# Cross-attention keys of a Perceiver layer: transposes on TensorE replaced by transposing DMA transfers

## Chip, core and metric

The kernel runs on one core of a Trainium2 chip. A core has five engines, each with its own instruction queue: TensorE (PE; its weight loads are listed as PEld), VectorE (DVE), ScalarE (ACT), GpSimd (POOL) and SyncE (SP), which here issues nearly all DMA transfers. Sixteen DMA engines move data between HBM, where the inputs lie, and SBUF, the on-chip memory of 128 partitions. TensorE writes to PSUM, eight banks of 128 x 512 float32. The metric is the device time of one execution in microseconds (us).

## The reference, cut to what matters

Everything is float32. `x` is (16, 64, 256), the context `cond` is (16, 1601, 256). A layer runs three residual parts: a block with self attention and cross attention, a second small block-local attention with its feed-forward, and a gated feed-forward. The change touches the cross attention of the first part:

```python
qx = _fp8_linear_pertensor(ln_out, wqx, wqx_scale, qx_in_scale).reshape(b, s, g, hpg, d)
qx = _ln(qx, qxln_w, qxln_b)
kvx = jnp.einsum('bsi,oi->bso', cond, w_kv_x)
kx, vx = jnp.split(kvx, 2, axis=-1)
kx = _ln(kx.reshape(b, sc, g, d), kxln_w, kxln_b)
vx = vx.reshape(b, sc, g, d)
xout = _gqa(qx, kx, vx).reshape(b, s, nh * d)
```

There are 16 query heads and g = 8 key groups of d = 128. `_ln` is a layer norm over d with weight and bias; `_gqa` is softmax(q k / sqrt(d)) v, two heads to a key group.

## The kernel before

**Tiles and units.** The 1,024 rows of `x` make 8 tiles of 128 rows, two batches each (`NT = 8`). The cross attention of one tile (i), one half of the key groups (hh, four of them) and one batch (bb) is a *unit*: 32 units in all. A unit walks through the 1,601 context rows in 13 chunks of 128 (`NC = 13`); the last one is a tail of 65, and the tails of both batches of a tile are projected together. `unit` (line 541) writes every step of a chunk as a small function and puts it into a heap with `at(step, rank, fn)`; the heap is then emptied in the order of (step, rank). Units start 13 steps apart, so that one step holds about one chunk of scores of one unit and one chunk of sums of the unit before it. Self attention, queries, output projections and the last two parts of the layer are generators, which are spawned at steps of their own, with waits in `PACE` and `SCHEDULE`. That gives the order of the program; the framework's planner then fills each engine's queue from it, by priority and by its own estimates of times. `behind` (line 493) adds an order between two VectorE instructions by hand.

**One chunk.** `load_T` loads context columns, two chunks at a time. `project` (line 564) makes keys of four groups, 128 x 512, in PSUM (`ps_k`; L568, two passes of two matmuls), and ScalarE squares them (L502). The weights have been centred, so the mean of a key is zero. `squares` sums the squares on VectorE (L507), then GpSimd adds epsilon (L190) and takes the power -0.5 (L191). `normalise` multiplies the keys by these roots on VectorE into SBUF (`kn`, L514). `transpose_k` turns the four 128 x 128 blocks on TensorE (L589, into `tr_kx`), and ScalarE copies them to SBUF as `kT`, with the layer norm's weight and bias, which are per partition there (L598). `score` multiplies with the queries `qx` (L606), ScalarE scales the scores into `P` (L611), and VectorE keeps a running maximum `M` (L616). At the unit's end `maximum` turns and reduces `M` (L623 to L633), and a DMA through a DRAM row brings it back to all partitions (`rowd`, L635, L652). About 18 steps after the first, the second half of a chunk's work starts: subtract the maximum (L656), exponential (L660), and `accumulate`, which multiplies the probabilities with the raw context (`ctxN`, L561; L675). The value projection follows later in `pair_out`.

**Queries.** `queries` (line 382) makes four heads of one tile at a time through `heads` (line 364): projection, layer norm, four transposes (L376), and one ScalarE pass with weight and bias into `qx` (L377).

**Other lines named below.** L897 is a GpSimd product in the last parts; L922 loads `near` keys there, 16 transfers in a row; L272 rounds weights at the start; L1062 is an activation of 128 columns with a scale per row; L368 copies a projection from PSUM.

Buffers: two PSUM tiles for projections (`mm`), three for scores, transposes and everything else (`s`), three for sums; three `kT`, 18 `P`, ten weight pieces (`w`).

Of the kernel before, what the change touches and what calls it, by code (L numbers as in the profile page):

```python
# [42 lines left out]
    0: (-9, [4, 11, 16, 25], [-3, -3, 11, 21]),  # L43
    1: (27, [36, 45, 61, 69], [37, 50, 62, 74]),
}
# [5 lines left out]
    "ln": [-1, 0.5, 0.5, -1, 1.5, -1.5, -4.5, 1.5],  # L51
    "last": [0, 0, 0, 0, 0, 0, 0, 2, -1, 0, 2, -1.5, -0.5, -0.5, -0.5, -0.5, 0, 0, 0, 0, 0.5, -0.5, -1, 1, 0, 0.5, -0.5, 0.5, -1, 0, 0, -1],
    "quarter": [-2, 3.5, 2, 1.5],
    "pair": [0, 0, 1, 1, 0, 1],
    "ln_first": [0, 0, 0, 1, 0, -0.5, -2.5, 1.5],
    "last_tile": [-1.5, 0.5, 0, 1, 0, 1.5, -2, -0.5, 0.5, 0.5, 0, 0.5, -1.5, 0.5, -0.5, 1, -1, 1, -0.5, 0, 0, 0, -1, 3, 0, 1.5],
}


# [12 lines left out]
def body(tc, ctx, a):  # L72
# [30 lines left out]
    def fact(*k):  # L103
        facts[k] = facts.get(k, 0) + 1
# [58 lines left out]
    pscale = const.tile([P, 1], F32, tag="pscale", name="pscale")  # L163
    V.tensor_tensor(pscale, col("p_in"), col("p_w"), ALU.mult)
    rows = const.tile([P, 3, H], F32, tag="rows", name="rows")
    shp = const.tile([P, 32 + 8], F32, tag="shp", name="shp")
# [149 lines left out]

    xqs, qxs = {}, {}

# [44 lines left out]

    def heads(xq, ws, scale, scale_sq, lw, lb, out_t):
        ps = s_tile("ps_q")
        project(ps, xq, ws, 0, 512)
        qn = qp.tile([P, 512], F32, tag="qn", name="qn")
        A.copy(qn, ps)  # L368
        yield 1
        st = norm_stats(qn, 4, D, scale=scale, scale_sq=scale_sq)  # L370
        yield 1
        norm_apply(qn, qn, st, 4, D)
        yield 1
        tr = tr_tile("tr_q")
        for h in range(4):
            PE.transpose(tr[:, h * P : (h + 1) * P], qn[:, h * P : (h + 1) * P], ident)  # L376
        A.activation(  # L377
            out_t().rearrange("p b h s -> p h b s"), tr.rearrange("p (h b s) -> p h b s", h=4, b=2),
            AF.Identity, bias=lb, scale=lw,
        )  # L380

    def queries(i, p):

        ws = weights("wqx", p) if i else [raw_piece("wqx", p)]
        yield 2
        if p % 2 == 0:
            qxs[i, p // 2] = qp.tile([P, 2, 8, S], F32, tag="qx", name="qx")
        out = qxs[i, p // 2]
        yield from heads(
            xqs[i][3], ws, col("wqx_s"), wsq[:, 3:4], col("qxln_w"), col("qxln_b"),  # L390
            lambda: out[:, :, 4 * (p % 2) : 4 * (p % 2) + 4, :],
        )
        fact("qx", i, p // 2)


# [97 lines left out]
    def behind(ins, other):  # L493
# [4 lines left out]
        )  # L498

    def square(ps, n):  # L500
        sq = one.tile([P, 512], F32, tag="sq", name="sq")
        A.activation(sq[:n], ps[:n], AF.Square)  # L502
        return sq

    def roots(sq, n):
        ss = small.tile([P, 4], F32, tag="ss", name="ss")
        mark["ss"] = V.reduce_sum(ss[:n], sq[:n].rearrange("p (g d) -> p g d", g=4), axis=AX.X)  # L507
        rs = small.tile([P, 4], F32, tag="rsx", name="rsx")
        rsqrt(rs[:n], ss[:n], 1.0 / D, 4)
        return rs  # L510

    def normalised(ps, rs, n):
        kn = one.tile([P, 512], F32, tag="kn", name="kn", bufs=2)
        mark["kn"] = V.tensor_tensor(  # L514
            kn[:n].rearrange("p (g d) -> p g d", g=4), ps[:n].rearrange("p (g d) -> p g d", g=4),
# [4 lines left out]
    def last_keys(hh):  # L520
# [12 lines left out]
        for g in range(4):  # L533
            PE.transpose(tr[:, g * P : g * P + B], kn[:B, g * D : (g + 1) * D], ident[:B, :B])
        A.activation(
            k_last[:, hh], tr.rearrange("p (g t) -> p g t", g=4)[:, :, 0:B],
            AF.Identity, bias=col("kxln_b"), scale=col("kxln_w"),
        )
        fact("k_last", hh)

    def unit(i, hh, bb, base):
        b = 2 * i + bb
        last = b == B - 1 and hh == 1
        st = {"cxT": {}, "cxN": {}, "ps": {}, "ss": {}, "rs": {}, "kn": {}, "kT": {}, "P": {}, "pT": {}}
        pair = pairs.setdefault((i, hh), {})
# [18 lines left out]
        def project(c):  # L564
            n, o = P, (c % 2) * P
            ps = ps_mm.tile([P, 512], F32, tag="mm", name="ps_k")
            for k in range(2):
# [3 lines left out]
                )  # L571
            st["ps"][c], st["ss"][c] = ps, square(ps, n)

        def squares(c):
            st["rs"][c] = roots(st["ss"].pop(c), P)

        def normalise(c):
            kn = normalised(st["ps"].pop(c), st["rs"].pop(c), P)

            for name in ("M", "mx"):  # L580
                if name in mark:
                    behind(mark["kn"], mark[name])
            st["kn"][c] = kn

        def transpose_k(c):
# [4 lines left out]
            if c < NC - 1:  # L590
                kT = st["kT"][c] = kp.tile([P, 4, P], F32, tag="kT", name="kT")
                out, src = kT, tr.rearrange("p (g t) -> p g t", g=4)
            else:
                need(1, "k_last", hh)
                kT = pair["kT"] = one.tile([P, 4, 2, TAIL], F32, tag="kT_tail", name="kT_tail")
                GP.tensor_copy(kT[:, :, :, REST], k_last[:, hh, :, b : b + 2])
                out, src = kT[:, :, :, 0:REST], tr.rearrange("p (g e t) -> p g e t", g=4, e=2)
            A.activation(out, src, AF.Identity, bias=col("kxln_b"), scale=col("kxln_w"))  # L598

        def score(c):  # L600
# [4 lines left out]
            for g in range(4):  # L605
# [3 lines left out]
                )  # L609
            pc = pp.tile([P, 512], F32, tag="P", name="P")  # L610
            A.activation(pc[:n], ps[:n], AF.Copy, scale=C_ATT)  # L611
            if c == 0:
                st["M"] = one.tile([P, 512], F32, tag="M", name="M")
                mark["M"] = V.tensor_copy(st["M"], pc)
            else:
                mark["M"] = V.tensor_tensor(st["M"][:n], pc[:n], st["M"][:n], ALU.max)  # L616
            st["P"][c] = pc

# [8 lines left out]

        def out_rows(r):

            tr = tr_tile("tr_r")  # L630
            PE.transpose(tr[0:4, 0:P], r, ident)
            rT = small.tile([4, P], F32, tag="rT", name="rT", bufs=2)
            A.copy(rT, tr[0:4, 0:P])  # L633
            d = dram.tile([4, P], F32, tag="rowd", name="rowd", bufs=4)
            nc.sync.dma_start(out=d, in_=rT)  # L635
            return d

        def maximum():
            r = turned("M", ALU.max)
            if not last:  # L640
                st["mxd"] = out_rows(r)
                return
# [11 lines left out]
        def exponent(c):  # L654
            n, pc = rows_of(c), st["P"][c]
            ins = V.tensor_tensor(pc[:n], pc[:n], st["mx"][:n].rearrange("p g q -> p (g q)"), ALU.subtract)  # L656
            for name in ("kn", "ss"):
                behind(ins, mark[name])
            mark["mx"] = ins
            A.activation(pc[:n], pc[:n], AF.Exp)  # L660
# [31 lines left out]
        def turn_contexts(k):  # L692
# [7 lines left out]
            fact("pc", i, hh)  # L700

        for c in range(NC):
            if c < NC - 1 or bb == 0:
                if c % 2 == 0:
                    at(base + c - 5, 0, lambda c=c: load_T(c))
                at(base + c, 1.1, lambda c=c: project(c))
                at(base + c, 6.2, lambda c=c: squares(c))
                at(base + c + 1, 2.5, lambda c=c: normalise(c))
                at(base + c + 1, 8.9, lambda c=c: transpose_k(c))
            at(base + c + 2, 8.9, lambda c=c: score(c))  # L710
            at(base + c + 17, 0, lambda c=c: load_N(c))
            at(base + c + 18, 8.4, lambda c=c: exponent(c))
            at(base + c + 20, 0.1, lambda c=c: accumulate(c))
        at(base + 15, 8.9, maximum)
        if not last:
            at(base + 17, 0.1, maximum_in)
        for k in range(2):
            at(base + 33, (1.6, 6.2)[k], lambda k=k: turn_contexts(k))

# [8 lines left out]

    FILL = {"pair": 5, "norm": 1, "sc0": 2, "sc1": 4, "av0": 1, "hn": 1, "quant2": 1, "xn": 1}

# [138 lines left out]
    def last_parts(i, start):  # L869
# [55 lines left out]
        def product(out, x, y, order):  # L925

            t = one.tile([P, 1024], F32, tag="b2b", name="prod")
            V.tensor_tensor(t.rearrange("p (h j d) -> p h j d", h=8, j=8), x, y, ALU.mult)
# [213 lines left out]
    for i in range(NT):  # L1142
        base = 52 * i
        for hh in range(2):
            for bb in range(2):
                unit(i, hh, bb, base + 26 * hh + 13 * bb)
            spawn(base + 26 * hh + 13 + 34 - 2 + (2, 2)[hh], 6.0, paced("pair", pair_out(i, hh, 3 if i < NT - 1 or hh == 0 else None)))
        ln0, sa0, qx0 = SCHEDULE[i] if i in SCHEDULE else (
            base - 22, [base + o for o in (-15, -2, 7, 21)], [base + o for o in (-17, -6, 11, 17)]
        )  # L1150
        spawn(ln0, 3.6, paced("ln" if i else "ln_first", ln_tile(i)))
        for p in range(4):
            spawn(sa0[p] - 2, 2.0, paced("sa", self_attention(i, p)))
            spawn(qx0[p] - 2, 4.0, paced("qx", queries(i, p)))
        l0 = base + {NT - 3: 96, NT - 2: 85, NT - 1: 79}.get(i, 91)
        spawn(l0, 0.6, paced("last" if i < NT - 1 else "last_tile", last_parts(i, l0)))
    spawn(60, 5.7, ternary())
# [76 lines left out]
```

## Time and profile before

| what | value |
|---|---|
| time, median of 2 runs | 2552.14 us (2551.69 to 2552.58) |
| profiled execution, time | 2552.61 us |
| its span on the core | 2550.8 us |
| granted TensorE clock, mean | 0.993 of full speed |
| transposes of keys on TensorE (L589) | 1,600, busy 241.0 us |
| scores (L606), full chunks | 3,072, busy 407.3 us |
| sums (L675) | 4,160, busy 807.6 us |
| projections (L568) | 1,600, busy 759.4 us |
| HBM read and written | 337.94 and 25.23 MB, 142 GB/s over the span |

How to read it: the busy time of an engine is the time in which at least one of its instructions was under way. A group's row gives its line, engine, operation, the names of what it writes and reads, shapes, count, busy time, mean ns of one instruction, and then the idle time of the engine just before them with what ended it. "Issue" is time in which an engine waited for nothing that the profile shows. The chain is the work that ended last, followed back from the last instruction. The sequencer's queue of an engine has a q behind its name (SPq). In the slices each digit is a tenth of busy share in one fortieth of the span.

### The profile page before, as it was taken

Reading aid. Unit: us, or ns where it says so; the run is one execution under the profiler, and the core shown is the slowest. Engines: PE = TensorE matmul, PEld = TensorE weight load, DVE = VectorE, ACT = ScalarE, POOL = GpSimd, SP = SyncE. Lnnn points to the kernel's source line nnn. Section 1 sums busy time; section 2 is a strip of 40 time slices with the busy share of each in tenths; the row PEclk is TensorE's granted clock in tenths of the full one; section 3 lists DMA queues with packets and bytes.
Section 4 is the critical chain, followed back from the end, with each engine's and each line's share of the span. In section 5 each row is a group of like instructions: output and inputs, shape, how many; then the busy total and the mean of one; then the engine's idle time right before and its main releaser. Section 6 shows DMA issues by size and latency. Waiting matters only on the chain.

```text
span 2550.8 us, 40365 instructions
## 1 busy us (share of the span) xinstructions
PE 2489.9 (98%) x14009; PEld 1927.3 (76%) x14009; DVE 1857.2 (73%) x4491; ACT 1327.9 (52%) x2444; POOL 944.0 (37%) x1225
## 2 busy tenths in 40 slices
PE   6999999999999999999999999999999999999995
PEld 3677777777777777877778777777777777777784
DVE  6777767678767786577866777677876777766755
ACT  3655545454574555645556554545454455555431
POOL 3434333343333433334333443334433343333300
PEclk8999999999999999999999999999999999999998
DMA  7655725434544354433543435343363334532333
GB/s 248 201 187 182 273 70 183 144 112 141 170 146 130 103 175 143 156 123 115 179 146 127 134 110 185 126 136 105 104 219 123 121 114 128 168 107 61 124 115 104
DMA packets 223587, 365.85 MB, mean 143 GB/s; under 512 B 31676, under 2 KB 159896, under 8 KB 223384
## 3 DMA queue, kind: packets, MB, share of 16 engines
q1 hardware_dynamic: 222840, 362.57, 43.3%
q8 instruction: 112, 1.84, 0.3%
q10 hardware_dynamic: 544, 0.69, 0.1%
q14 instruction: 91, 0.75, 0.1%
HBM read 337.94 MB, written 25.23 MB: 142 GB/s over the span
## 4 chain that ended last, share of the span: by engine, by line
PE 83%; DVE 9%; POOL 4%; DMA 1%; issue 1%; ACT 1%; SPq 1%; DVEq 0%; POOLq 0%; ACTq 0%
PE acc L675 25%; PE ps_k L568 23%; PE s L606 12%; PE tr_kx L589 6%; PE po_p L309 2%; PE ps_q L358 2%; PE po_x L746 2%; POOL rsx L191 2%; POOL ve L190 1%; DVE ss L507 1%; PE tr_pc L698 1%; PE sc L440 1%; DVE kn L514 1%; PE ps_kv L358 1%; PE pgu L1058 1%
## 5 line engine op out<-in xcount | busy, mean ns | idle before, releaser
L675 PE MATMUL acc<-ctxN,P 128*128 128x257 f32 (+5 forms) x4160 | 807.6, 340 | 0.1
L568 PE MATMUL ps_k<-wkx,ctxT 128*128 128x512 f32 x1600 | 759.4, 596 | 9.8 <-DVE wkx L1129 6.8
L675 PEld LDWEIGHTS acc<-ctxN,P 128*128 128x128 f32 (+1 forms) x4160 | 689.6, 190 | 84.5 <-issue 14.3
L190 POOL TENSOR_SCALAR ve<-ss 128x4 f32<-128x4 f32 (+1 forms) x418 | 253.3, 606 | 1281.0 <-DVE ss L507 1079.6
L502 ACT ACTIVATE sq<-ps_k 128x512 f32<-128x512 f32 x402 | 240.1, 597 | 692.7 <-PE ps_k L568 688.1
L191 POOL TENSOR_TENSOR rsx<-ve,nhalf 128x4 f32<-128x4 f32 x402 | 484.3, 1205 | 31.6
L606 PEld LDWEIGHTS s<-qx,kT 128*128 128x128 f32 x3072 | 387.5, 192 | 61.9 <-issue 51.7
L568 PEld LDWEIGHTS ps_k<-wkx,ctxT 128*128 128x128 f32 x1600 | 274.3, 192 | 201.5 <-issue 188.7
L514 DVE TENSOR_TENSOR kn<-ps_k,rsx 128x512 f32<-128x512 f32 x402 | 275.8, 686 | 193.6 <-POOL rsx L191 191.9
L606 PE MATMUL s<-qx,kT 128*128 128x128 f32 x3072 | 407.3, 275 | 0.0
L507 DVE TENSOR_REDUCE ss<-sq 128x4 f32<-128x512 f32 x402 | 273.7, 681 | 156.0 <-ACT sq L502 153.4
L660 ACT ACTIVATE P<-P 128x512 f32<-128x512 f32 (+1 forms) x416 | 261.4, 630 | 137.0 <-DVE P L656 135.8
L611 ACT ACTIVATE P<-s 128x512 f32<-128x512 f32 (+1 forms) x416 | 248.1, 596 | 146.2 <-PE s L606 138.6
L598 ACT ACTIVATE kT<-tr_kx,vec 128x512 f32<-128x512 f32 x384 | 296.7, 773 | 7.7 <-PE tr_kx L589 7.7
L656 DVE TENSOR_TENSOR P<-P,mx 128x512 f32<-128x512 f32 (+1 forms) x416 | 282.3, 680 | 0.0
L616 DVE TENSOR_TENSOR M<-P,M 128x512 f32<-128x512 f32 (+1 forms) x384 | 261.8, 682 | 15.7 <-ACT P L611 15.0
L589 PE MATMUL tr_kx<-ident,kn 128*128 128x128 f32 x1600 | 241.0, 273 | 8.3 <-DVE kn L514 4.1
L589 PEld LDWEIGHTS tr_kx<-ident,kn 128*128 128x128 f32 x1600 | 187.7, 142 | 11.5 <-issue 5.1
L209 DVE TENSOR_SCALAR qn<-qn,mv,rs 128x128 f32<-128x128 f32 x256 | 73.9, 342 | 84.0 <-POOL rs L203 83.9
L191 POOL TENSOR_TENSOR rs<-ve,nhalf 128x4 f32<-128x4 f32 (+2 forms) x144 | 116.0, 806 | 8.9
L190 POOL TENSOR_SCALAR ve<-mv,wsq 128x4 f32<-128x4 f32 (+1 forms) x96 | 38.1, 397 | 127.8 <-DVE mv L200 127.6
L309 PE MATMUL po_p<-wproj,cat 128*128 128x256 f32 x512 | 83.5, 306 | 0.6 <-ACT qn L368 0.5
(203 smaller groups left out, 2439.9 us busy)
## 6 DMA issues: line engine op xcount, KB each, us to landing
wproj<-wproj SPq DMA_DIRECT2D x120, 512.0 KB
ctxT<-in_ctx SPq DMA_DIRECT2D x192, 256.0 KB
ctxN<-in_ctx_n SPq DMA_DIRECT2D x384, 128.0 KB
wq<-wq SPq DMA_DIRECT2D x56, 512.0 KB
wkv<-wkv SPq DMA_DIRECT2D x56, 512.0 KB
wqx<-wqx SPq DMA_DIRECT2D x56, 512.0 KB
near<-kv SPq DMA_DIRECT2D x248, 64.0 KB
wvx<-in_w_kv_x SPq DMA_DIRECT2D x16, 512.0 KB
```

What stands on the lines that cost most here:

```text
L190: GP.tensor_scalar(ve[:n, :g], in_, scale, EPS, ALU.mult, ALU.add)
L191: GP.tensor_tensor(out, ve[:n, :g], nhalf[:n, :g], ALU.pow)
L507: mark["ss"] = V.reduce_sum(ss[:n], sq[:n].rearrange("p (g d) -> p g d", g=4), axis=AX.X)
L514: mark["kn"] = V.tensor_tensor(kn[:n].rearrange("p (g d) -> p g d", g=4), ps[:n].rearrange("p (g d) -> p g d", g=4), rs[:n].unsqueeze(2).t ...
L568: PE.matmul(ps[:n, :], lhsT=st["cxT"][c // 2][:, k, o : o + n], rhs=wkx[:, k, 512 * hh : 512 * (hh + 1)], start=k == 0, stop=k == 1,)
L589: PE.transpose(tr[:, g * P : (g + 1) * P], kn[:, g * D : (g + 1) * D], ident)
L598: A.activation(out, src, AF.Identity, bias=col("kxln_b"), scale=col("kxln_w"))
L606: PE.matmul(ps[:n, g * P : (g + 1) * P], lhsT=kT[:, g, 0:n], rhs=qxs[i, hh][:, bb, 2 * g : 2 * g + 2, :].rearrange("p h s -> p (h s)"), st ...
L616: mark["M"] = V.tensor_tensor(st["M"][:n], pc[:n], st["M"][:n], ALU.max)
L656: ins = V.tensor_tensor(pc[:n], pc[:n], st["mx"][:n].rearrange("p g q -> p (g q)"), ALU.subtract)
L660: A.activation(pc[:n], pc[:n], AF.Exp)
L675: PE.matmul(ps, lhsT=pc[:n, g * P : (g + 1) * P], rhs=cx[:n, o : o + w], start=g == 2 and c == 0, stop=c == NC - 1 and (g, o) in ((2, 0), ...
```

## The change

Keys are no longer normalised and turned on the way to the scores. For all units but the first and the last (`DIRECT = (1, 1)`), the raw projected keys are copied from PSUM as two planes of 16-bit halves (`split_keys`, ScalarE), stored to DRAM (`store`, 256 KB a chunk), and loaded back by a transposing DMA (`turn`, 256 KB), which writes both halves beside each other, so that the result read as float32 is the turned key. Projections of these units run one step earlier (`LEAD = 1`), tails three. The first and last unit copy the raw keys and turn them on TensorE as before. Since keys are raw, the roots multiply the scores: ScalarE's copy of 512 columns becomes four of 128 columns with a scale per row. The tail is still normalised, then split and turned by DMA (15 of 16).

The key weight goes into the queries' layer norm (`qk`), and the key bias becomes a term per query: `biases` computes it from the normalised queries (a GpSimd product, a VectorE sum), `out_rows` turns it to rows and stores it to DRAM (32 times), and `bias_in` spreads it over partitions once per unit. `biased` adds it to every chunk of scores on GpSimd, before the running maximum, which gets a function and a later step of its own. The roots' epsilon is scaled so that 1/sqrt(d) is in the power. `ordered` replaces `behind` for chains of instructions on VectorE and GpSimd. Steps, ranks, `PACE` and `FILL` are set anew, and the tile `prod` of the last parts moves into the buffers of weight pieces.

```diff
+DIRECT, LEAD = (1, 1), 1
@@ constants
+    qk = const.tile([P, 2], F32, tag="qk", name="qk")
+    V.tensor_scalar(qk, vec[:, _COLS["qxln_w"].start : _COLS["qxln_b"].stop], col("kxln_w"), None, ALU.mult)
+    def bias_rows():
+        t = quant_tile()[:, 0 : 3 * D]
+        nc.sync.dma_start(out=t.rearrange("p (r d) -> p r d", r=3), in_=a["qrows"].partition_broadcast(P))
+        yield 1
...
@@ queries
+        def biases(qn):
+            t = quant_tile()
+            GP.tensor_tensor(
+                t.rearrange("p (h d) -> p h d", h=4), qn.rearrange("p (h d) -> p h d", h=4),
+                brow.unsqueeze(1).to_broadcast([P, 4, D]), ALU.mult,
+            )
+            V.reduce_sum(qs, t.rearrange("p (h d) -> p h d", h=4), axis=AX.X)
+            V.tensor_scalar(qs, qs, bsum, None, ALU.add)
...
+        out_rows(qs, qbs[i, p // 2][4 * (p % 2) : 4 * (p % 2) + 4, :])
@@ roots
-        rsqrt(rs[:n], ss[:n], 1.0 / D, 4)
+        ve = small.tile([P, 4], F32, tag="vx", name="vx")
+        ordered("pool", GP.tensor_scalar(ve[:n], ss[:n], D * EPS, None, ALU.add))
+        ordered("pool", GP.tensor_tensor(rs[:n], ve[:n], nhalf[:n, 0:4], ALU.pow))
@@ unit
             st["ps"][c], st["ss"][c] = ps, square(ps, n)
+            if c < NC - 1:
+                split_keys(c, ps) if lead else plain_keys(c, ps)
...
+        def split_keys(c, src):
+            t = st["kh"][c] = kp.tile([P, 2, 512], U16, tag="kh", name="kh", bufs=2)
+            A.copy(t, src.bitcast(U16).rearrange("p (c e) -> p e c", e=2))
+        def store(c):
+            d = st["kd"][c] = dram.tile([P, 2, 512], U16, tag="kd", name="kd", bufs=3)
+            nc.sync.dma_start(out=d, in_=st["kh"].pop(c))
+        def turn(c):
+            t = kT_tile()
+            nc.sync.dma_start_transpose(out=t, in_=st["kd"].pop(c).rearrange("k e c -> (k e) c"))
+            st["kT"][c] = as_keys(t)
...
-            A.activation(pc[:n], ps[:n], AF.Copy, scale=C_ATT)
...
+            rs = st["rs"].pop(c)
+            for g in range(4):
+                A.activation(pc[:, g * P : (g + 1) * P], ps[:, g * P : (g + 1) * P], AF.Copy, scale=rs[:, g : g + 1])
+        def biased(c):
+            n, pc = rows_of(c), st["P"][c]
+            qb = st["qb"].rearrange("p h s -> p (h s)")
+            ordered("pool", GP.tensor_tensor(pc[:n], pc[:n], qb[:n], ALU.add))
...
+        lead = 0 if u < DIRECT[0] or u >= 4 * NT - DIRECT[1] else LEAD
...
-                at(base + c, 1.1, lambda c=c: project(c))
-                at(base + c, 6.2, lambda c=c: squares(c))
-                at(base + c + 1, 2.5, lambda c=c: normalise(c))
-                at(base + c + 1, 8.9, lambda c=c: transpose_k(c))
-            at(base + c + 2, 8.9, lambda c=c: score(c))
+                s = base + c - lead - (2 if tail and lead else 0)
...
+                at(s, 4, lambda c=c: project(c))
+                at(s, 4.2, lambda c=c: squares(c))
+                if tail:
+                    at(s + 1, 1, lambda c=c: normalise(c))
+                if lead:
+                    at(s + 1 + tail, 0.9, lambda c=c: store(c))
+                    at(s + 2 + tail, 0.8, lambda c=c: turn(c))
+                    if tail:
+                        at(s + 4, 1.5, lambda c=c: tail_keys(st["kT"].pop(c)))
+                else:
+                    at(s + 1, 6, lambda c=c: transpose_k(c))
+            lag = max(0, 4 - c // 2) if soon else 0
+            at(base + c + 2 + lag, 8.5, lambda c=c: biased(c))
+            at(base + c + 3 + lag, 4.5, lambda c=c: running(c))
+            at(base + c + 2, 5.5, lambda c=c: score(c))
...
-        at(base + 15, 8.9, maximum)
+        at(base + 15, 5.5, maximum)
@@ last parts
-            t = one.tile([P, 1024], F32, tag="b2b", name="prod")
+            t = wp.tile([P, 1024], F32, tag="w", name="prod")
```

## The prediction

> **What bounds the kernel now.** I read the page from the top: engine totals, slices, chain.
>
> ```profile
> span 2550.8 us, 40365 instructions
> PE 2489.9 (98%) x14009; PEld 1927.3 (76%) x14009; DVE 1857.2 (73%) x4491; ACT 1327.9 (52%) x2444; POOL 944.0 (37%) x1225
> PEclk8999999999999999999999999999999999999998
> DMA  7655725434544354433543435343363334532333
> q1 hardware_dynamic: 222840, 362.57, 43.3%
> PE 83%; DVE 9%; POOL 4%; DMA 1%; issue 1%; ACT 1%; SPq 1%; DVEq 0%; POOLq 0%; ACTq 0%
> ```
>
> TensorE (PE) is busy for 98% of the span, at full granted clock from slice 2 on, and holds 83% of the chain. DMA is well filled early (0.5 to 0.7 in most of the first ten slices), half that later. A busy PE need not be a PE at its peak, so I looked at the chain piece by piece, mid-kernel:
>
> ```profile
> 1210.54 0.89 PE s L606 x8
> 1211.43 0.44 PE tr_kx L589 x4
> 1211.86 1.75 PE acc L675 x10
> 1213.61 1.72 PE ps_k L568 x4
> 1215.33 0.94 PE ps_q L358 x4
> ```
>
> Each piece starts where the last ended. Scores: 8 instructions of 128 columns in 0.89 us, 0.111 each; projection: 4 of 512 columns in 1.72, 0.43 each. Time goes with columns: PE does nothing but stream. What leaves PE's queue here comes off the end, until something else is late. A transposed chunk costs 0.44 us there (the 273 ns of one transpose in its row overlap its neighbours). There are 416 steps (32 units of 13 chunks), 6.13 us each.
>
> Prices for the rest, groups by shape:
>
> ```profile
> L589 PE MATMUL tr_kx<-ident,kn 128*128 128x128 f32 x1600 | 241.0, 273 | 8.3 <-DVE kn L514 4.1 <-DVE am L845 1.7 <-DVE mv L200 1.3
> L598 ACT ACTIVATE kT<-tr_kx,vec 128x512 f32<-128x512 f32 x384 | 296.7, 773 | 7.7 <-PE tr_kx L589 7.7
> L514 DVE TENSOR_TENSOR kn<-ps_k,rsx 128x512 f32<-128x512 f32 x400 | 274.4, 686 | 192.0 <-POOL rsx L191 190.2
> L611 ACT ACTIVATE P<-s 128x512 f32<-128x512 f32 x384 | 229.1, 597 | 140.3 <-PE s L606 132.8
> L1062 ACT ACTIVATE sgc<-pgu,vec 128x128 f32<-128x128 f32 x16 | 5.5, 366 | 12.1 <-PE pgu L1058 12.0
> L272 ACT CAST w_hi<-wproj 128x1024 fp32r<-128x1024 f32 x8 | 8.3, 1043 | 0.0
> L897 POOL TENSOR_TENSOR r<-qk,shp 128x512 f32<-128x512 f32 x8 | 12.1, 1507 | 14.1 <-ACT qk L885 14.1
> ```
>
> **PE.** 360 full chunks (30 units; the first and last stay on PE) and 15 tails lose four transposes each: 375 x 0.4375 us = 164. The chain gives L589 6.0% of the span, 153 us for 400 chunks, 143 for 375; I take 164, since between 300 and 2400 us its share is 6.8%. Added: one 4-row transpose per query piece, 32 x 0.18 (the L631 piece of the chain) = 6. Net -158: 2552.6 of the profiled execution (span 2550.8 and 1.8 around it) becomes 2394.6. The profiled time lies 0.5 above the median shown, so nothing is corrected.
>
> **ScalarE.** Per moved chunk: L598 goes (-0.773); the split into 16-bit planes writes 1,024 elements, priced as L272 (+1.04); the scores' one copy becomes four 128-column ones with a scale column (4 x 0.366 from L1062, -0.597: +0.867). Sum +1.13 x 360 = 409. The 24 direct chunks add about 30, tails 13, the query rows 8 (32 x 0.253 of L633): 1328 becomes 1788, 75% of 2395. Bounds on the split, which reads every second half-word of PSUM, as no row does: 0.585 us (the 512-element copy L368) to twice L272; ScalarE then has 1624 to 2163, 68 to 90%. I take L272, nearest in element count. It stays under PE, but a ps_k buffer is now freed by ScalarE after 0.60 + 1.04 us rather than by VectorE at the end of squares, sum, power and product (3.8 us): that relieves PE. A score buffer is held 1.46 instead of 0.60, against one score-buffer allocation per chunk saved: even.
>
> **VectorE, GpSimd.** VectorE loses 384 x 0.686 = 263 and gains 30 for query sums: 1857 to 1624, 68%. GpSimd gains the bias on 416 chunks and 32 query products at 1.508: 944 to 1620, 68%. Both stay hidden under PE while the handovers fit. The longest handover is at a unit's end: four score copies 1.46, bias 1.51, maximum 0.68, 3.7 us, before PE turns the maximum about one step (5.75 us) later. If each of 32 ends came 1 us late: 32 us. I put 10 in.
>
> **DMA.** All queues have 43.8% of 2550.8 = 1117 us of 16 engines. A store of the planes is 128 rows of 2 KB; such packets took 103.6 ns here, so 128 x 103.6 / 16 = 0.83 us, times 375 = 311. Bias rows: 32 of the same size, 27. So 1455 without the transposing transfers, of which this trace has none. Bounds by its own packets: 1,024 source rows of 256 B at 18.6 ns (8,192 such packets ran) / 16 = 1.19 us; destination columns of 32 B, 8,192 per transfer, at the 10.6 ns of 64 B packets: 5.4 us. A price below plain copying has no reason, so no gain.
>
> Here the Trainium skill speaks on both sides. "VectorE: DVE Perf Modes", The three transpose paths, sets 1309 ns for a 128x128 16-bit turn by DMA against 390 on TensorE: eight such blocks a chunk, 10.5 us one after another, 3927 us in all. "DMA: Bandwidth & Descriptors", Latency and other measured facts, has 261 GB/s for a non-contiguous case: 1.0 us a chunk, 377 in all. The first is one small turn, [...]the second is a rate and lies by the 256 B row. I take 1.19: 446 us, DMA 1901 of 2395, 79%. PE ceases to be the bound at (2395 - 1455) / 375 = 2.5 us a transfer; break-even is (2553 - 1455) / 375 = 2.93.
>
> Early there is little room. One step's store and turn are 2.02 of 5.75 us, 35%, on top of this:
>
> ```profile
> 255.00:319.00 64.00, 63.95 (x376) 50.38 (x376) 50.19 (x121) 37.66 (x76) 24.11 (x30) 1.00 0.79 272
> ```
>
> (window, length, busy of PE, PEld, DVE, ACT, POOL with counts, clock, DMA share, GB/s). 0.79 + 0.35 = 1.14: 9 us over; the windows before stand at 0.55 to 0.61 and reach 0.96. I put 12 in for the first 320 us.
>
> **SyncE's queue and the new waits.** Each turn waits in SP's queue for its own store to land; behind it stand the next context loads, weights and the next store, and PE waits for those last. SP's waits now (who for whom: total us, times, longest):
>
> ```profile
> SPq L561 <- PE acc L675: 1034.5, 363, 6.4
> SPq L652 <- DMA rowd<-rT: 12.7, 13, 2.1
> SPq L922 <- DMA kv<-r: 12.5, 8, 2.7
> ```
>
> L561 is slack: SP waits for buffers, running ahead of PE. The two below price a landing at 2.1 to 2.7. A step on SP then costs 2.7 of wait, one ctxN issue 0.33, half a ctxT 0.19, store 0.38, turn 0.59 (as L922, the costliest issue; bounds 0.33 and its longest, 1.47), other loads 0.5 (some 460 issues of 0.4 over 416 steps): 4.7 of 5.75 us. It fits, narrowly. The 16 near-key issues of 0.59 (9.4 us), twice a tile, push turns back. The slack of a turn: its score comes 3.15 steps, 18 us, after its projection; matmul and split take 3, the store's landing 2.5, the turn's own 3.5; 9 us are left, won back at 1 us a step. 16 bursts at 0 to 5 us: 0 to 80; I take 1 each, 16, since the planner spreads them among other loads. The product tile that moves into the ten weight buffers costs nothing while SP is ahead, and falls under the same 16 if it isn't. Start-up's extra row load and retuned ranks: 2.
>
> Sum: 2394.6 + 10 + 12 + 16 + 2 = 2435.
>
> **Rivals.**
> A (forecast, 0.56): PE stays the bound, 2395 to 2500, likeliest 2435. For it: PE's gapless chain and no other engine above 79%.
> B (0.12): the freed time is eaten by handovers, within 2%. Split at its upper price (ScalarE 90%), unit ends 32, bursts 80: 2395 + 32 + 80 + 30 for ScalarE at 90% = 2537. For it: ScalarE's four short copies sit between score and bias. Against: step-long distances.
> C (0.32, slower): transposing transfers set the pace. Mechanism: sixteen engines are held longer per transfer than source rows explain, because its destination is 32-byte pieces in 128 partitions. It decides from 2.93 us a transfer; at 4 us 1455 + 1500 = 2955, at 5.4 us 3490. For it: the small-packet prices, the skill's 1309 ns, and SP's narrow fit, which a slower landing breaks too. Against: the skill's rate.
> That the change doesn't do what it says (PE still turning keys) would show in L589's count and stay at 2552; I fold it into B.
>
> **Numbers.** Faster by over 2% (what a measurement of this kernel can tell from no change; under 2501) 0.56, within 0.12, slower 0.32. A's own range is 2395 to 2500. The range for 8 in 10 must reach into C: about 0.14 of its 0.32 lies below 2955 (4 us a transfer), so 2390 to 2955 leaves out about 0.18 above.
>
> **What would show it.** Right: the remaining key transposes number 100 in PE's groups; PE stays near 97% busy with scores and projections back to back; DMA share near 0.79; the split near 1.04 us and four score copies near 0.37; GpSimd's bias near 1.5; SP waiting about 2 us for each store. Wrong by C: DMA share at 0.9 or more in all slices, PE waiting for kT at the scores, PE under 90%, and a packet price for turns well above 18.6 ns per 256 B. Wrong by B: PE waiting for ScalarE's P copies, or for the maximum. What would spoil the forecast unseen is a planner that orders queues by a landing time for turns that the chip doesn't keep.

## The result and the profile after

The changed kernel takes 2673.62 us (2673.0 to 2674.25) against 2552.14: ratio 1.0476, interval 1.0431 to 1.0521. It is slower by 4.8%, where 4.6% faster was forecast. The profiled execution took 2673.0 us, its span is 2671.2.

The page of the changed kernel, the rows that answer to those shown of before (engine totals; granted clock and DMA share in forty slices; main DMA queue; chain by engine):

```profile
span 2671.2 us, 40721 instructions
PE 2439.1 (91%) x12541; PEld 1812.4 (68%) x12541; DVE 1753.0 (66%) x4175; ACT 1608.1 (60%) x3667; POOL 1543.6 (58%) x1673
PEclk9899999999899999999999999999989999999998
DMA  7689998876897677985879867887678866995333
q1 hardware_dynamic: 706520, 567.91, 76.5%
PE 46%; DVE 23%; POOL 15%; ACT 6%; DMA 5%; issue 4%; SPq 1%; DVEq 0%; POOLq 0%; ACTq 0%
```

No engine is full any more. PE falls from 98% to 91% and from 83% to 46% of the chain; VectorE and GpSimd rise from 13% to 38% of it. DMA is busy at 0.77 of the span, as forecast, but not full. The mean granted clock fell from 0.993 to 0.963.

Where the span went, from these pages: it grew by 120 us. PE's idle time (span less busy) rose from 60.9 to 232.1, by 171. PE's busy time fell by only 51, from 2489.9 to 2439.1, though its transposes are gone (100 of 1,600 are left) and a few row transposes came, -158 us by the prediction's sum. So the work that stayed takes 107 us longer. The lower clock accounts for 81 of these: 0.037 x 2671 = 99 us against 0.007 x 2551 = 18. The other 26 are not assigned.

The new operations of the compute engines cost about what was set down for them (groups by shape of the changed kernel):

```profile
L704 POOL TENSOR_TENSOR P<-P,qb 128x512 f32<-128x512 f32 x384 | 498.8, 1300 | 246.8 <-ACT P L699 246.3
L699 ACT ACTIVATE P<-s,rsx 128x128 f32<-128x128 f32 x1536 | 444.8, 379 | 74.0 <-PE s L689 72.4 <-PE tr_aq L962 1.0
L644 ACT COPY kh<-ps_k 128x1024 uint16<-128x1024 uint16 x360 | 363.5, 1010 | 6.3 <-DMA kd<-kh 6.2
```

GpSimd's bias takes 1.30 us (1.51 assumed), a score copy 0.379 (0.366), the split 1.01 (1.04). So what was missed is not the price of one of these instructions, but waits. Who waited for whom in the changed kernel (total us, times, longest), first PE and its loads:

```profile
PE acc L760 <- ACT P L745: 79.9, 46, 5.0
PEld acc L760 <- ACT P L745: 108.3, 73, 5.4
```

Then SP's queue, which waits for a store to land before it issues the turn (L658), and for the split before it issues the store (L648):

```profile
SPq L658 <- DMA kd<-kh: 471.4, 263, 5.2
SPq L648 <- ACT kh L644: 201.8, 113, 6.9
```

PE's longest wait in total is for the exponential of old scores (L745), not for turned keys; the times of PE and of its loads overlap in part. One such place, the chain of the changed kernel in order of time (start, us, what; "..." marks lines left out):

```profile
1210.00 1.54 DVE kn L226 x2
...
1213.49 0.59 DVE ss L556
1214.09 0.60 DVE M L713
1214.69 0.61 DVE P L743
1215.32 0.64 ACT P L745
1215.96 0.04 issue
1216.01 2.01 PE acc L760 x6
```

VectorE works through its queue in a fixed order: a norm, small steps of the last parts, sums, the maximum, then the subtraction (L743) that the exponential and PE wait for. The norm came late because it needs GpSimd's roots, and then it was slow: its two instructions took 1.54 us where two undisturbed ones take about 0.68 (341 ns each). In that time GpSimd ran a bias addition (start, us, what):

```profile
1209.81 1.40 POOL L704 TENSOR_TENSOR P<-P,qb 128x512 f32<-128x512 f32 x1
```

The last section comes back to this. PE was idle for 3.43 us before 1216.01. What follows is in the windows of that place (window, length, busy of PE, PEld, DVE, ACT, POOL with counts, clock, DMA, GB/s):

```profile
1210.00:1217.00 7.00, 3.57 (x20) 2.45 (x20) 5.65 (x15) 1.80 (x4) 3.94 (x4) 1.00 0.54 138
1217.10:1220.50 3.40, 3.40 (x10) 2.18 (x9) 1.35 (x3) 2.01 (x4) 3.11 (x4) 0.51 0.33 114
```

After the gap the clock is halved for 3.4 us, and one chunk's projection takes 2.75 us instead of 1.88. The trace records 34 such stretches in the changed kernel and 4 before. The Trainium skill has this rule ("TensorE: Matmul & The Clock Gate", What's actually happening: after an idle window of about 3.4 us the clock is halved). The trace agrees on the length: 20 of the 34 stretches last 3.41 us. But the window before need not be idle throughout: the gap here ended at 1216.01 and the clock fell at 1216.99, so in the 3.41 us ahead of the drop PE idled for 2.43. The price is what the mean clock gives, 81 us more than before.

### The profile page after: what moved, and what is told of

Read it like the earlier page. It is cut to its first block, busy times and chain, and to the rows that moved or that the text cites. A ratio compares the mean times of both kernels' runs of the same rounds, so it can differ in the third digit from the quotient of the medians.

```text
span 2671.2 us, 40721 instructions
## 1 busy us (share of the span) xinstructions
PE 2439.1 (91%) x12541; PEld 1812.4 (68%) x12541; DVE 1753.0 (66%) x4175; ACT 1608.1 (60%) x3667; POOL 1543.6 (58%) x1673
## 4 chain that ended last, share of the span: by engine, by line
PE 46%; DVE 23%; POOL 15%; ACT 6%; DMA 5%; issue 4%; SPq 1%; DVEq 0%; POOLq 0%; ACTq 0%
PE acc L760 15%; PE ps_k L617 14%; PE s L689 6%; POOL P L704 4%; POOL rsx L561 3%; POOL rs L208 3%; DMA kd<-kh 3%; DVE M L713 3%; DVE ss L556 2%; POOL vx L560 2%; DVE P L743 2%; DVE qn L226 2%; ACT P L699 1%; ACT sq L551 1%; PE po_p L326 1%
## 5 line engine op out<-in xcount | busy, mean ns | idle before, releaser
L760 PE MATMUL acc<-ctxN,P 128*128 128x257 f32 (+5 forms) x4160 | 858.6, 352 | 80.4 <-ACT P L745 79.9
L760 PEld LDWEIGHTS acc<-ctxN,P 128*128 128x128 f32 (+1 forms) x4160 | 715.8, 197 | 210.7 <-ACT P L745 108.3
L704 POOL TENSOR_TENSOR P<-P,qb 128x512 f32<-128x512 f32 (+1 forms) x416 | 539.5, 1298 | 252.1 <-ACT P L699 246.3
L560 POOL TENSOR_SCALAR vx<-ss 128x4 f32<-128x4 f32 x402 | 262.3, 653 | 594.5 <-DVE ss L556 543.2
L561 POOL TENSOR_TENSOR rsx<-vx,nhalf 128x4 f32<-128x4 f32 x402 | 495.0, 1231 | 33.1
L745 ACT ACTIVATE P<-P 128x512 f32<-128x512 f32 (+1 forms) x416 | 265.6, 639 | 389.9 <-DVE P L743 388.8
L699 ACT ACTIVATE P<-s,rsx 128x128 f32<-128x128 f32 x1536 | 444.8, 379 | 74.0 <-PE s L689 72.4
L644 ACT COPY kh<-ps_k 128x1024 uint16<-128x1024 uint16 x360 | 363.5, 1010 | 6.3 <-DMA kd<-kh 6.2
L743 DVE TENSOR_TENSOR P<-P,mx 128x512 f32<-128x512 f32 (+1 forms) x416 | 283.1, 682 | 1.9 <-ACT mx L735 1.9
L226 DVE TENSOR_SCALAR qn<-qn,mv,rs 128x128 f32<-128x128 f32 x256 | 97.2, 432 | 98.6 <-POOL rs L220 98.6
L326 PEld LDWEIGHTS po_p<-wproj,cat 128*128 128x128 f32 x512 | 67.5, 190 | 6.8 <-ACT sq L551 2.8
L216 DVE BATCH_NORM_STATS2 st<-qn 128x6 f32<-128x128 f32 x256 | 63.6, 269 | 8.2 <-ACT qn L385 8.2
L412 POOL TENSOR_TENSOR q_y<-qn,brow 128x512 f32<-128x512 f32 x32 | 47.1, 1472 | 29.6 <-DVE qn L226 26.1
```

The source lines that it names most:

```text
L560: ordered("pool", GP.tensor_scalar(ve[:n], ss[:n], D * EPS, None, ALU.add))
L561: ordered("pool", GP.tensor_tensor(rs[:n], ve[:n], nhalf[:n, 0:4], ALU.pow))
L644: A.copy(t, src.bitcast(U16).rearrange("p (c e) -> p e c", e=2))
L699: A.activation(pc[:, g * P : (g + 1) * P], ps[:, g * P : (g + 1) * P], AF.Copy, scale=rs[:, g : g + 1])
L704: ordered("pool", GP.tensor_tensor(pc[:n], pc[:n], qb[:n], ALU.add))
L760: PE.matmul(ps, lhsT=pc[:n, g * P : (g + 1) * P], rhs=cx[:n, o : o + w], start=g == 2 and c == 0, stop=c == NC - 1 and (g, o) in ((2, 0), ...
```

## Experiments

All ratios are to the kernel before, run beside it. PE idle is span less busy; clock loss is one less the mean clock, times the span. Both are in us and from the profiled execution. The three versions with a plain load or without transfers leave the turning out, so their scores are other numbers: they serve for timing alone.

| kernel | us | ratio (interval) | PE idle | clock loss |
|---|---|---|---|---|
| before | 2552.14 | 1 | 61 | 18 |
| changed | 2673.62 | 1.0476 (1.0431 to 1.0521) | 232 | 99 |
| no bias | 2555.26 | 1.0013 (1.0000 to 1.0026) | 151 | 74 |
| all keys on PE | 2700.45 | 1.0581 (1.0565 to 1.0597) | 149 | 40 |
| bias on VectorE | 2560.34 | 1.0036 (1.0021 to 1.0051) | 153 | 64 |
| plain load | 2641.48 | 1.0352 (1.0337 to 1.0368) | 210 | 92 |
| no bias, all on PE | 2569.40 | 1.0069 (1.0052 to 1.0086) | 60 | 13 |
| maximum before bias | 2611.96 | 1.0230 (1.0201 to 1.0260) | 197 | 84 |
| no bias, 3 plane buffers (3PB) | 2535.86 | 0.9935 (0.9914 to 0.9956) | 145 | 56 |
| no bias, 3PB, early maximum | 2559.27 | 1.0035 (1.0021 to 1.0048) | 171 | 64 |
| no bias, 3PB, lead 2 | 2529.01 | 0.9903 (0.9888 to 0.9918) | 137 | 56 |
| no bias, 3PB, lead 2, late turns | 2505.85 | 0.9813 (0.9782 to 0.9844) | 127 | 53 |
| no bias, no transfers | 2422.86 | 0.9489 (0.9475 to 0.9504) | 80 | 19 |
| no bias, 3PB, lead 2, late turns, 4 key buffers | 2538.90 | 0.9948 (0.9932 to 0.9964) | 137 | 76 |
| no bias, idle additions | 2575.96 | 1.0101 (1.0084 to 1.0118) | 164 | 82 |
| no bias, 3PB, lead 2, late turns, plain load | 2471.44 | 0.9685 (0.9669 to 0.9701) | 112 | 32 |

In the cuts of code "..." marks lines left out. Two theories stood at the start. *Handover*: GpSimd's bias stands between score and maximum, VectorE's order puts the subtractions behind the maximum, PE starves. *DMA*: turned keys and loads come late.

**No bias.** A term per query is the same for every key, and softmax drops it, so it can be left out altogether:

```diff
-            lambda: out[:, :, 4 * (p % 2) : 4 * (p % 2) + 4, :], biases,
+            lambda: out[:, :, 4 * (p % 2) : 4 * (p % 2) + 4, :],
...
-        out_rows(qs, qbs[i, p // 2][4 * (p % 2) : 4 * (p % 2) + 4, :])
...
-        at(base + (3.9 if soon else 1), 0.7, bias_in)
...
-            at(base + c + 2 + lag, 8.5, lambda c=c: biased(c))
...
```

> The changed kernel without the bias term of the queries: no GpSimd product and row store per query piece, no bias load, no GpSimd addition to the 416 chunks of scores. A term per query is the same for every key, so softmax cancels it. Handover theory (PE starves because subtraction and exponential queue behind a running maximum that waits for GpSimd's bias, and the clock drops with it): 2440 to 2520 us, PE's wait for the exponential (188 us on PE and PEld) falls below 60. DMA theory (turned keys and loads come late because the DMA queues are full): GpSimd's work isn't the limit, 2620 to 2670 us, PE's busy share stays near 91%.

2555.26 us: 118 us of the loss were the bias. The waits for the exponential fell as the handover theory says (the same views of this kernel):

```profile
PE acc L755 <- ACT P L740: 11.6, 14, 1.7
PEld acc L755 <- ACT P L740: 29.1, 36, 1.8
```

What now stands out are scores that wait for a buffer that ScalarE empties, and for turned keys:

```profile
PE s L684 <- ACT P L694: 30.9, 8, 5.8
PE s L684 <- DMA kT<-kd: 19.7, 17, 3.0
```

But PE's saving did not come out: the time lies between the two ranges, at that of the kernel before. A second cause was left.

**All keys on PE.**

```diff
-DIRECT, LEAD = (1, 1), 1
+DIRECT, LEAD = (32, 0), 1
```

> The changed kernel with all units as its first and last one: keys turned on TensorE, no stores to DRAM and no transposing transfers, roots on the scores and bias from the queries as in the change. DMA theory: PE gets its 164 us of transposes back and the waits go, 2560 to 2590 us. Handover theory: the waits for the exponential stay, the transposes fill a part of them, 2640 to 2720 us.

2700.45 us. Without a single store or turn of keys the kernel is slower still, by 149 us against before. The DMA theory as the main cause falls; moving the turning to DMA even gains 27 us here.

**Bias on VectorE.**

```diff
-            ordered("pool", GP.tensor_tensor(pc[:n], pc[:n], qb[:n], ALU.add))
+            ordered("dve", V.tensor_tensor(pc[:n], pc[:n], qb[:n], ALU.add))
```

> The changed kernel with the addition of the bias to the scores on VectorE instead of GpSimd, in the same place of the order. VectorE gets 416 x 0.68 = 283 us more (76% of the span), GpSimd 540 less. Handover theory with GpSimd as the slow link: 2540 to 2620 us. If the length of the chain and not GpSimd's share in it counts: 2640 to 2700. DMA theory: 2660 to 2690.

2560.34 us: 113 of the 118 us come back although the addition, its bias rows and its place in the order are all still there. It is GpSimd's part in the chain that costs, not the chain's length in steps. The run doesn't part the two ways in which GpSimd could cost: its slower, later result, and its hold on VectorE.

**Plain load.** Keys are stored and loaded back with the same bytes, but not turned, and the halves keep their order:

```diff
-            A.copy(t, src.bitcast(U16).rearrange("p (c e) -> p e c", e=2))
+            A.copy(t.rearrange("p e c -> p (e c)"), src.bitcast(U16))
...
-            nc.sync.dma_start_transpose(out=t, in_=st["kd"].pop(c).rearrange("k e c -> (k e) c"))
+            nc.sync.dma_start(out=t.rearrange("p g t -> p (g t)"), in_=st["kd"].pop(c).rearrange("k e c -> k (e c)"))
```

> The changed kernel with a plain load in place of the transposing transfer, and the 16-bit halves left in their order: the same bytes to and from DRAM, the keys not turned, so the scores are other numbers. Rates: 2 KB rows instead of 256 B rows free about 0.7 us of 16 engines a chunk, 270 us in all. DMA theory: 2500 to 2580 us. Handover theory: 2640 to 2670 us.

2641.48 us, 32 less: turning as such is a small part of the changed kernel's time.

**No bias, all on PE.** The edits of the first two runs together.

> No bias term (as the first run) and all keys turned on TensorE, so no stores and no transposing transfers. Beside the first run (2555 us) it gives the worth of the DMA path where the bias is not in the way. If the path is worth PE's 164 us less what late stores cost: 2620 to 2680 us. If the path is worth little because its waits eat PE's saving: 2560 to 2590 us.

2569.40 us, inside the second case's range: the waits eat PE's saving. With this the four corners stand: bias or none, DMA or PE (us).

| | with bias | no bias | bias costs |
|---|---|---|---|
| turned on PE | 2700.45 | 2569.40 | 131 |
| turned by DMA | 2673.62 | 2555.26 | 118 |
| DMA path gains | 27 | 14 | |

The two effects add up to within 13 us. The bias costs as much where PE keeps all its transposes, so it is not the thinner PE that uncovers it. In the run without bias and with all keys on PE, PE is 98% busy, at a clock of 0.995, with the four score copies in place: roots on the scores cost little (2569 against 2551 beside it, new ranks included). And the DMA path gains 14 to 27 us where 158 us of PE's work go.

**Maximum before bias.** The running maximum reads the scores as ScalarE left them; GpSimd does the same work after it.

```diff
-            at(base + c + 2 + lag, 8.5, lambda c=c: biased(c))
-            at(base + c + 3 + lag, 4.5, lambda c=c: running(c))
+            at(base + c + 2 + lag, 8.4, lambda c=c: running(c))
+            at(base + c + 2 + lag, 8.5, lambda c=c: biased(c))
```

> The changed kernel with the running maximum taken from the scores before GpSimd adds the bias (a maximum only shifts the softmax, so any near value serves), one step part earlier; GpSimd does the same work. If VectorE's maximum, waiting for GpSimd in a fixed order, is what holds the exponentials up: 2540 to 2600 us. If GpSimd simply has too much to do in some stretches: 2640 to 2680 us.

2611.96 us, between the two: 62 us come back. About half of the bias's price goes with the maximum that waits for it. The edit also moves the maximum to an earlier place, which by itself cost 23 us in a kernel without the bias (early maximum, below), so 62 is a net figure.

**No bias, idle additions.** The first run plus 416 GpSimd additions of the same size, in the bias's place, on a tile `spare` that nothing else uses.

```diff
...
+            at(base + c + 2 + lag, 8.5, lambda c=c: ordered("pool", GP.tensor_tensor(spare[: rows_of(c)], spare[: rows_of(c)], spare[: rows_of(c)], ALU.add)))
```

> The first run (no bias, 2555 us) plus 416 GpSimd additions of the bias's size and in its place, on a spare tile that nothing else reads or writes. If GpSimd's occupied time and its reading beside VectorE cost time by themselves: 2590 to 2630 us. If only the dependence of maximum and exponential on the bias costs: 2550 to 2570 us.

2575.96 us, 21 above the first run, below the range for occupied time and above that for dependence alone. So of 118 us, some 21 are GpSimd's occupied time with its hold on VectorE, and 62 go with the maximum. The rest, 35, would be the exponentials' own dependence; the parts were not taken from one kernel, so that rest is a difference and not shown by itself.

**Three plane buffers.** In the first run ScalarE waited 83 us for stores to free a plane buffer, and its score copies stood behind.

```diff
...
-            t = st["kh"][c] = kp.tile([P, 2, 512], U16, tag="kh", name="kh", bufs=2)
+            t = st["kh"][c] = kp.tile([P, 2, 512], U16, tag="kh", name="kh", bufs=3)
...
```

> The first run (no bias) with three buffers for the split planes instead of two. There ScalarE waited 83 us in all, up to 7 us at once, for a store to free a buffer, and scores queued behind it. If that wait passes on to PE: 2490 to 2530 us. If the next limit is elsewhere (the store's landing in SP's queue, loads): 2545 to 2560 us.

2535.86 us, 19 less, between the cases; ScalarE's wait fell to 21.5 us.

**Early maximum.** As that run, with `running` at step `base + c + 2`, rank 8.4.

> As the run before (no bias, three plane buffers), with the running maximum in the same step as its scores, as the kernel before has it, since no bias stands between. If the late maximum still holds exponentials up (58 us of waits of PE and its loads for the exponential and more behind): 10 to 40 us below the run before. Else the same within 10 us.

2559.27 us, 23 above: a miss. The late maximum was not in the way once the bias was gone, and the other order was worse.

**Lead 2, then late turns.** Both without bias and with three plane buffers. First `LEAD = 2`; then each turn one step later, so that its store has landed when SP reaches it.

```diff
-DIRECT, LEAD = (1, 1), 1
+DIRECT, LEAD = (1, 1), 2
```

```diff
-                    at(s + 2 + tail, 0.8, lambda c=c: turn(c))
+                    at(s + 3 + tail, 0.8, lambda c=c: turn(c))
...
-                        at(s + 4, 1.5, lambda c=c: tail_keys(st["kT"].pop(c)))
+                        at(s + 5, 1.5, lambda c=c: tail_keys(st["kT"].pop(c)))
```

> No bias, three plane buffers, and projections, stores and turns of the moved units one more step ahead of their scores (lead 2). If scores still wait for turned keys that land late (15 us on PE directly, more through ScalarE): 2500 to 2525 us. If the stores' landing in SP's queue is the trouble, lead alone changes little: 2525 to 2545 us.

> As the run before, with each turn issued one step later, two steps after its store, so that SP no longer waits for the store to land (646 us of waits in the run with three plane buffers). If that wait delays the loads and stores queued behind it, and PE through them: 2470 to 2515 us. If SP had time to spare: as the run before within 10 us.

2529.01 and 2505.85 us. The lead gives 7, which the spread of the two kernels' times (2528.7 to 2540.8, 2525.1 to 2531.2) doesn't tell clearly from nothing; the late turns give 23. SP's wait for stores (the turn is L653 in these kernels), in the runs with three plane buffers, with lead 2, with late turns, and with late turns and more key buffers (below), in this order:

```profile
SPq L653 <- DMA kd<-kh: 646.5, 310, 5.2
```

```profile
SPq L653 <- DMA kd<-kh: 305.0, 179, 4.3
```

```profile
SPq L653 <- DMA kd<-kh: 190.6, 112, 4.8
```

```profile
SPq L653 <- DMA kd<-kh: 509.3, 209, 5.4
```

The total of SP's wait is no measure of the gain: the lead alone took 341 us off it for 7 us of time, the late turns another 114 for 23. That the stores' landing was the cause of the 23 is thus likely, not shown.

2505.85 us beats the kernel before by 1.9% (interval 1.6 to 2.2) and the changed one by 168 us.

**More key buffers.** Four `kT` buffers instead of three, five DRAM tiles instead of three.

> The version with lead 2 and late turns (2506 us), with four buffers for turned keys instead of three and five DRAM tiles instead of three. There SP's turns still waited some 240 us for the scores and whatever PE did before them to free a key buffer, with stores and loads queued behind. If those waits reach PE: 2475 to 2495 us. If SP has slack now and only the fuller DMA queues and the low clock after short gaps are left: 2496 to 2512 us.

2538.90 us, 33 above: a miss, and telling. With buffers free, the planner put many turns early in SP's queue again, close behind their stores, and SP's wait rose from 191 to 509 us (last line above). The traces show the order: counted in transfers that SP issues, a turn stands three behind its store in the median with three plane buffers, four with lead 2, six with late turns, and three again here. The step in the program is the same in the last two; so it seems that the lack of buffers had kept the turns late. Two counts of buffers were changed at once, so which of them did it is open.

**No transfers.** The first run once more (no bias), but the split copy goes straight into the buffer that the scores read, five of them; no store and no turn, keys not turned.

```diff
-            t = st["kh"][c] = kp.tile([P, 2, 512], U16, tag="kh", name="kh", bufs=2)
-            A.copy(t, src.bitcast(U16).rearrange("p (c e) -> p e c", e=2))
+            t = kT_tile()
+            A.copy(t.rearrange("p g t -> p (g t)"), src.bitcast(U16))
...
-                    at(s + 1 + tail, 0.9, lambda c=c: store(c))
-                    at(s + 2 + tail, 0.8, lambda c=c: turn(c))
```

> No bias, and the split copy goes straight into the buffer that the scores read, in its own order: no store, no transposing transfer, keys not turned (the scores are other numbers). PE has 164 us less to do than before and nothing to wait for from DMA. If the transfers and SP's waits are what ate PE's saving: 2400 to 2440 us at a clock near 0.99. If a thinner PE merely uncovers the other engines' handovers: 2480 to 2530 us, with the clock near 0.97.

2422.86 us, as the first case said. Its page:

```profile
span 2420.5 us, 38491 instructions
PE 2340.9 (97%) x12509; PEld 1765.1 (73%) x12509; DVE 1614.1 (67%) x4108; ACT 1595.9 (66%) x3635; POOL 993.4 (41%) x1225
PEclk9999999999999999999999999999999999999998
```

PE's saving is real and nearly all of it comes out when nothing is handed to DMA: 147 us below the version without bias that turns all keys on PE (2569.40), of 158 set down, with PE 97% busy and the clock at 0.992. The transfers cost 2555 - 2423 = 132 us in the kernel without bias.

**Late turns, plain load.** The plain load's edit on the version with late turns.

> The version with lead 2 and late turns (2506 us), with plain loads in place of the transposing transfers and the halves left in order: same bytes, keys not turned, so other scores. If the transposing as such (256-byte packets, 1.23 us of issue on SP) is most of what is left above 2423 us: 2430 to 2460 us. If it is the traffic and the waits of a store and a load: 2475 to 2505 us.

2471.44 us, between the cases: of the 83 us that part the best version from the one without transfers, 34 are the turning as such and 49 a store and a load of the same bytes, with their waits. "As such" has two parts that this pair of runs doesn't separate: smaller packets, and SP's time to issue, 1.25 us for a turn against 0.33 for a plain load (medians).

## Why the prediction was wrong

Without bias and transfers the kernel takes 2423 us, the transfers add 132 and the bias 118: together (rounded) the 2674 of the changed kernel. The forecast had 2397 for the first, 12 + 16 for the second and 10 for the third.

**Right.** PE as the bound before, the worth of its transposes (floor 2394.6; the kernel without transfers reaches 2422.9 with 80 us idle), the prices of the compute instructions above. The trace shows a turn as 1,024 packets of 256 B and none of 32 B. Packets of 256 B took 24.1 ns in the mean where I took 18.6, so a turn holds the engines for 1,024 x 24.1 / 16 = 1.54 us instead of 1.19, about half of the break-even of 2.93. The row was the nearest price. Of the estimates from the Trainium skill, 1309 ns a block ("VectorE: DVE Perf Modes", The three transpose paths) made it 10.5 us, and 261 GB/s ("DMA: Bandwidth & Descriptors", Latency and other measured facts) made it 1.0; 256 KB in 1.54 us are 170 GB/s. Rival C, which carried all of my slower chance, did not happen. A slower kernel came by a mechanism of rival B's kind, which I had closed at 2537 us.

**Right by luck, or off without harm.** The range of 2390 to 2955 holds the measured time, but it reaches so far only for rival C. The DMA share (0.79 forecast, 0.77 measured) agrees because the span grew too: the engines were busy for 2054 us, not 1901, and 131 of the difference are the dearer turns. ScalarE came to 1608 us where 1788 were forecast, mostly because the four score copies of a chunk overlap: 444.8 us for 384 chunks are 1.16 each, not 4 x 0.366 = 1.46.

**The step that failed: handovers.** I wrote "Both stay hidden under PE while the handovers fit", named only the one at a unit's end, and put 10 us in. GpSimd's bias costs 118 to 131 us, and it acts on every chunk: 62 us go with the maximum in VectorE's fixed order, 21 with GpSimd's occupied time, and 35 no run assigns. Busy shares of 68%, as forecast for both engines, said nothing of it; nor did the sum have a term for VectorE's instructions that GpSimd holds up (last section). The prediction should have listed, for the new operation, what is queued behind it on GpSimd (roots of norms) and what behind its reader on VectorE (the subtraction, and through it PE's sums).

**The second: SP's queue.** I wrote "It fits, narrowly", with 4.7 of 5.75 us a step, and put in 16 us for SP's bursts and 12 for full DMA engines early. The transfers cost 132 us in the kernel without bias: 19 through ScalarE's plane buffers (not in the sum at all), 7 by the lead, 23 by the late turns, 34 for the turning as such, 49 for the rest of the traffic. These are successive differences along one line of versions. The first three are no larger than what a planner's reordering of queues moved in other runs (23 and 33 us), so only the total is firm. The wait for a store had been priced too high, at 2.7 us each (471 us over 263 waits in the changed kernel are 1.8), the turn's issue too low, at 0.59 where it is 1.23 in the median; a sum of SP's own time did not price what stands behind a wait in its queue.

**The third: the clock.** The sum held PE's pace fixed. Here gaps of a few us also halved the clock after them: 81 us of the loss, which are contained in the 118 and 132 above. So each us of added gap cost about half as much again (171 us of idle, 81 of clock).

The assumption that the bias was needed also went untested: the term is the same for all keys of a query, and leaving it out is worth more than any other edit here that still computes the layer.

## What to carry to other kernels

A full PE does not hide a new handover: here the bias cost 131 us even where PE kept all its transposes. So follow each new operation to the queue it stands in and to the engine that reads its result in fixed order, and price waits a chunk, not a unit. A store that is read back belongs at a distance in the issuing queue, and the distance has to be checked there: the same step in the program gave six transfers or three, as the planner found buffers free. And a term that is constant over the softmax axis needs no engine at all.

## What the runs showed of the hardware

VectorE instructions are held up by GpSimd's additions. These are one group on VectorE before and after the change:

```profile
L223 DVE TENSOR_SCALAR q_yb<-q_y 128x512 bf16<-128x512 f32 x64 | 26.7, 417 | 0.3
```

```profile
L240 DVE TENSOR_SCALAR q_yb<-q_y 128x512 bf16<-128x512 f32 x64 | 40.0, 625 | 0.8
```

In the changed kernel 32 of the 64 began while a bias addition ran and took 830 ns in the mean, the other 32 took 419; for the 128-column normalisation of the queries (L226) it is 1145 ns against 348. Summed over VectorE's groups, the instructions that started under an addition took 94 us longer than their like. With the idle additions the same group takes 588 ns, with the bias on VectorE 418. The idle additions settle that this is no matter of waiting for data, since nothing depends on them: VectorE's 4,108 instructions are busy for 1694.6 us beside them and for 1622.1 in the first run. The Trainium skill has the rule ("SBUF — State Buffer", Who interferes with whom: VectorE's two-port modes and GpSimd exclude each other for a whole instruction). These rows agree with it, though the trace doesn't show in which mode an instruction ran.
